# Layer 2 of a two-layer cross-attention: where partial sums are added, how the image part joins the heads, and which function tables ScalarE uses

## The chip, the cores and the metric

The kernel runs on one core of a Trainium2 chip. The core has TensorE (PE in the profile; its weight loads are a row of their own, PEld), VectorE (DVE), ScalarE (ACT), GpSimd (POOL) and SyncE (SP, which here only issues DMAs). [...] The metric is the device time of one execution in microseconds. Three runs of the kernel before took 1663.47, 1673.33 and 1674.31 us, median 1673.33.

## The reference

Two attention layers follow each other, on 16 batches of 256 tokens with 320 channels, 20 heads of 16, and a context of 256 tokens with 512 channels, whose last tokens are the image tokens (four of them in layer 2). The change concerns layer 2:

```python
probs_t = softmax(q @ k_text.T * attn_scale)           # per head
text_out = probs_t @ v_text
qsem = probs_t @ text_ehs                              # 512 wide, per head and token
qsem = qsem / max(norm(qsem), EPS)
sem = qsem @ (ip_ehs / max(norm(ip_ehs), EPS)).T
probs_ip = softmax(q @ k_ip.T * attn_scale + 0.5 * sem)
out = text_out + (probs_ip * spatial_mask) @ v_ip
out = out @ W_out + b_out + residual
```

The norm of `qsem` is never formed from its 512 columns. With the Gram matrix G of the context (context times its transpose) the squared norm is p' G p for a row p of probabilities. The kernel computes that form.

## The kernel before, in words

All matrix products run in fp32r. Where more precision is wanted a value is split into a rounded part (made by an ACT copy) and a rest (made by a DVE or POOL subtraction), and products of the parts are summed; `halves` and `split` do this. Layer 1 runs in slots 0 to 79, layer 2 in slots 80 to 159, one slot for four heads of one batch, five slots per batch. `slot1(k)` writes the work of a slot in layer 2 for PE by hand: scores and transposed scores of two halves of the tokens (`both1`, L775 and L780), the norm (`norm1`, L814), the sums over tokens (`attend1`, L826 and L828), the maxima (`maxima1`, L792). Between these, `fill` issues steps of background tasks whose times are due: keys, values and Gram blocks of a coming batch (`keys1`, `tokens1`), its queries (`open1`), and for a finished batch the image softmax (`image_softmax`) and the output projection (`close1`, which calls `finish`). A task is a generator; each `yield` ends a step, and a list of times in slots says when each step is due. PE runs exactly in the order written. The order on the other engines is made by a list scheduler at build time, within the dependencies.

The places that matter:

- *Norm.* For each slot and each of two pairs of heads (u = 0 and 1) `rounded1` leaves the rounded exponentials in `ctb` (ACT, L804) and P minus that in `wt` (POOL, L805). `norm1` multiplies Gram blocks by the rounded part into a PSUM bank, in two groups n = 0 (four matmuls) and n = 1 (three), and DVE multiplies the bank by `wt` into `wt` (L816). After n = 1 the two products are added in SBUF (L818), by POOL for u = 0 and by DVE for u = 1. One slot later `attend1` sums them over tokens with a matmul by a column of ones (L828), behind the value products (L826), into the same bank.
- *Score maxima.* DVE takes the maximum of each score row (L781); the next score matmuls (L780) need that bank again, and L792 turns the maxima for the subtraction inside the exponentials' matmul.
- *Image part.* After a batch's last slot `gather` transposes the heads' results into `hT`, 128 x 3 x 256, and `image_softmax` prepares the image probabilities: a logarithm and an exponential (L897, L898) for the reciprocal root, POOL sums (L902 to L909), a DVE maximum (L907), another exponential (L911). `close1` multiplies them by the image values in three matmuls (L936); DVE adds each into `hT` (L937). Then `split` makes the rounded part of all 768 columns in one ACT copy (L511), the rest of the first 512 in one DVE subtraction (L512), and with one DVE multiply-add (L513) the last 256, whose channels 64 to 127 hold the rest of channels 0 to 63. The output projection (L522) reads the five pieces.
- *Gram block.* `tokens1` builds the blocks of G once per batch; block 5 is scaled by two on DVE (L489).
- *Tables.* ACT loads a function table when a function is not in the loaded set. Before, this stands ahead of a logarithm (L897) and again ahead of the exponential after it (L898).

PSUM tiles of the tags "X", "T" and "P" (at most three, two and one at a time) share six banks; which bank a tile gets is settled at build time.

Of the kernel before, what the change touches and what calls it, by code (L numbers as in the profile page):

```python
# [9 lines left out]
FR = mybir.dt.float32r  # L10
AF = mybir.ActivationFunctionType
ALU = mybir.AluOpType
# [4 lines left out]
B = 16  # L17
S = 256
# [30 lines left out]
def xattn2(  # L49
# [27 lines left out]
    nc = tc.nc  # L77
# [21 lines left out]
    def buf(tag, shape, dtype=F32, bufs=1, name=None):  # L99
        if tag in ("wB", "wD", "vr", "raw"):  # L100
            return sb.tile(shape, dtype, tag=tag, name=name or tag, bufs=bufs)
        size = 1
        for d in shape[1:]:
            size *= d
        if tag not in slots:
            slots[tag] = [0, dtype] + [const_tile([128, max(size, words.get(tag, 0))], f"{tag}_{i}", dtype) for i in range(bufs)]
        n, kind, *ring = slots[tag]
        assert kind == dtype and len(ring) == bufs, tag
        slots[tag][0] += 1
        t = ring[n % bufs][: shape[0], :size]  # L110
        names = "abcd"[: len(shape) - 1]
        if len(names) > 1:
            t = t.rearrange(f"p ({' '.join(names)}) -> p {' '.join(names)}", **dict(zip(names, shape[1:])))
        return t
# [17 lines left out]
    def queued(inst, *behind):  # L132

        for other in behind or [anchors.get(inst.ins.engine)]:
            if other is not None:
                tc.add_manual_dep(
                    inst.ins, other.ins.name, mybir.DependencyInfo(mybir.DependencyClass.NoSync, mybir.DependencyReason.DATA), reason="order"
                )
        return inst
# [225 lines left out]
    def weights1():  # L365


        cipn = buf("rawc", [128, 512], bufs=2, name="cipn")[:BI]
        dma(cipn, cip_d)
        yield  # L370
        sq = buf("rawc", [128, 512], bufs=2, name="sq")[:BI]
        nc.vector.tensor_mul(sq, cipn, cipn)
        nrm = rn[:BI, 0:1]
        nc.vector.tensor_reduce(nrm, sq, axis=AX.X, op=ALU.add)
        yield
        nc.scalar.activation(nrm, nrm, AF.Sqrt)
        yield
        nc.vector.tensor_scalar_max(nrm, nrm, 1e-12)
        nc.vector.reciprocal(nrm, nrm)
        dg = buf("rawc", [128, 512], bufs=2, name="dg")[:BI]  # L380
        nc.vector.memset(dg[:, BI : BI + 128], 1.0)
        nc.vector.tensor_scalar_mul(dg[:, :BI], ident[:BI, :BI], nrm)
        yield
        rp = bank()
        mm(rp[:, :BI], dg[:, BI : BI + 128], dg[:, :BI], start=True, stop=True)
        nc.vector.tensor_copy(rn, rp[:, :BI])
        cip = w1["cip"] = buf("kst", [128, 2, 4, BI], FR, bufs=SIZES["KST"], name="cip")
        raw = buf("rawc", [128, 4, BI], bufs=2, name="cipT")
        dma(raw, cipT_d.rearrange("(k p) n -> p k n", p=128))
        yield  # L390
        halves(cip[:, 0], cip[:, 1], raw, nc.vector, True)
        yield
# [69 lines left out]
    def tokens1(b):  # L462
        ct = ct1[b]
        V, G = v1t[b % 2], gmt[b % 2]
        vc = vcols(V, V1W)
        for t, lo, sc in ((0, 0, 1.0), (1, DUP, tmask[:, 2:3])):
            vp = bank()[:, :320]
            prod(vp, lambda s, k: ct(s, k)[:, lo : lo + 128], w1["v"], 4)
            nc.scalar.activation(vc[:, t, :, 0:16], vp.rearrange("p (h d) -> p h d", d=D), AF.Copy, scale=sc)
            yield  # L470
        rnb = rn[:, 4 * b : 4 * b + 4].unsqueeze(1).to_broadcast([128, H, NIP])
        for t, lo in ((0, 0), (1, DUP)):
            g = bank()[:, :S]
            prod(g, lambda s, k: ct(s, k)[:, lo : lo + 128], ct, 4)
            ip = g[:, T1:S].unsqueeze(1).to_broadcast([128, H, NIP])
            if t == 0:
                nc.vector.tensor_mul(vc[:, 0, :, 17:21], ip, rnb)
                nc.scalar.copy(G[:, 0, :], g[:, 0:128])
                nc.scalar.copy(G[:, 1, 4:], g[:, 128:T1])
                nc.vector.tensor_sub(G[:, 4, :], g[:, 0:128], f(G[:, 0, :]))  # L480
            else:
                tm = tmask[:, 2:3]
                nc.vector.scalar_tensor_tensor(vc[:, 1, :, 17:21], ip, tm, rnb, op0=ALU.mult, op1=ALU.mult)
                nc.scalar.activation(G[:, 2, :], g[:, 0:128], AF.Copy, scale=tm)
                nc.scalar.activation(G[:, 3, 4:], g[:, 128:T1], AF.Copy, scale=tm)
                nc.vector.scalar_tensor_tensor(
                    G[:, 5, :], g[:, 0:128], tm, f(G[:, 2, :]), op0=ALU.mult, op1=ALU.subtract
                )
                nc.vector.tensor_scalar_mul(G[:, 5, :], f(G[:, 5, :]), 2.0)  # L489
                nc.vector.scalar_tensor_tensor(  # L490
                    G[:, 6, 4:], g[:, 128:T1], tm, f(G[:, 3, 4:]), op0=ALU.mult, op1=ALU.subtract
                )
            yield
        return V, G
# [12 lines left out]
    def split(src, neg, eng, tag):  # L507

        hl = buf(tag, [128, 5, S], FR)
        order = queued if tag == "hq" else lambda inst: inst  # L510
        order(nc.scalar.copy(hl[:, 0:3], src))  # L511
        order(eng.tensor_sub(hl[:, 3:5], src[:, 0:2], f(hl[:, 0:2])))  # L512
        order(nc.vector.scalar_tensor_tensor(hl[:, 2], f(hl[:, 2]), neg, src[:, 2], op0=ALU.mult, op1=ALU.add))  # L513
        return hl
# [226 lines left out]
        return hT  # L741

    def finish(l, b, hT, resid, extra=None):
        if extra is not None:
            yield from extra(hT)
        if l:
            yield
        hh = split(hT, tmask[:, 6:7], nc.vector, "ho")
        results["taken", l * B + b] = True
        yield  # L750
        y = resid

        def evac(m, pp):
            nc.vector.scalar_tensor_tensor(
                y[:, m], pp, bo[:, l, m : m + 1], resid[:, m], op0=ALU.add, op1=ALU.add
            )

        yield from project(l, wo[l], hh, evac)
        return y
# [49 lines left out]
    def norm1(k, u, n):  # L809

        gm = get("t1", k // NG - B)[1]
        yp = bank().rearrange("p (h t) -> p h t", h=2)
        for i, (gb, kt) in enumerate(blocks[n]):
            mm(yp, gm[:, gb], R[k, u][:, kt], start=i == 0, stop=i == len(blocks[n]) - 1)  # L814
        w = W[k, u]
        nc.vector.tensor_mul(w[:, n], yp, w[:, n])  # L816
        if n:
            (nc.vector if u else nc.gpsimd).tensor_add(w[:, 0], w[:, 0], w[:, 1])  # L818

    def attend1(k):  # L820
        b, g = divmod(k - NS, NG)
# [108 lines left out]
    def close1(b):  # L930
        hT, (pT, bd) = results["gathered", 1, b], get("i1", b)

        def extra(hT):
            for p in range(3):
                ip = bank()[:, :S]
                mm(ip, bd[:, p * 128 : (p + 1) * 128], pT, start=True, stop=True)  # L936
                nc.vector.tensor_add(hT[:, p], hT[:, p], ip)  # L937
                yield

        y = yield from finish(1, b, hT, load(x1d[b], "xc"), extra)  # L940
        dma(out_d[b].rearrange("(k p) t -> p k t", p=128), y)
# [25 lines left out]
    def task(key, times, make, *needs):  # L967
        tasks[key] = [times, 0, make, needs, len(tasks)]
# [38 lines left out]
    def shifted(n, *times):  # L1007

        return [RAMP(n + t) for t in times]
# [23 lines left out]
    for b in range(B):  # L1033
        n = NS + 5 * b
        task(("k1", b), shifted(n, -7, -6.67, -6.33, -5.67, -5, -4.67), lambda b=b: keys1(b), ("w2",), *([("t1", b - 1)] if b else []), *([("w4", 1)] if b > 2 else []))
        task(("t1", b), shifted(n, -3.67, -3, -2.67, -2.33), lambda b=b: tokens1(b), ("k1", b), ("w3", b % 2))
        task(("o1", b), shifted(n, -7.67, -7, -6.67, -5.33, -4.33, -4), lambda b=b: open1(b), ("w7",), ("c0", b), *([("o1", b - 1)] if b else []))
        task(("i1", b), shifted(n, 6.67, 6.67, 6.67, 6.67, 7.33, 7.33, 7.67, 7.67, 8, 8.33), lambda b=b: image_softmax(b, NG - 1 if b == B - 1 else 0), ("gathered", 1, b), ("taken", B + b - 1), *([("i1a",)] if b == B - 1 else []))
        task(("c1", b), shifted(n + (1.67 if b > B - 3 else 0), 8.67, 8.67, 8.67, 8.67, 9, 9.67, 11.67, 13), lambda b=b: close1(b), ("i1", b), ("w4", 1))
    task(("i1a",), [2 * NS + 0.1], lambda: image_softmax(B - 1, 0, NG - 1), ("i1", B - 2))  # L1040
    spread = lambda t, d, n: [t + d * i for i in range(n)]
    thirds = lambda n, t: [t + i // 3 + (0.2, 0.6, 1.0)[i % 3] for i in range(n)]
# [153 lines left out]
```

## Time and profile before

| | |
|---|---|
| runs | 1663.47, 1673.33, 1674.31 us (median 1673.33) |
| profiled execution, span from first to last instruction | 1663.4 us |
| matmul busy / weight-load busy | 1533.5 us / 1222.9 us |
| DVE / POOL / ACT busy | 1317.2 / 1202.2 / 877.7 us |
| mean granted TensorE clock | 0.974 |

The profiled execution's own time is its span and some tenth of a microsecond: it agrees with the lowest of the three runs. Rows by line give the engine, the operation, output and input tiles, shapes and count, then busy time and the mean duration in ns, then the idle time of the engine just ahead of them and what ended it. Waits read "who, waiting for whom: total us, times, longest". Matmul ends are modelled, so a busy PE may hide short stalls. The first instruction of layer 2's norm runs at about 770 us; from there to about 1600 us the work repeats with each batch.

### The profile page before, as it was taken

To read this page: it belongs to the slowest core of one execution; us is meant where nothing else is said; L and a number is where in the kernel's file an instruction comes from. 1 tells how busy PE (TensorE), PEld (TensorE's weight loads), DVE (VectorE), ACT (ScalarE), POOL (GpSimd) and SP (SyncE) were. 2 spreads that over 40 slices of the span, in tenths; PEclk is the share of its full clock that TensorE was granted. 3 is DMA by queue.
4 is the path that set the end of the run, shared out by engine and by line. 5 is a ranking of instruction groups with operands and counts; after the bars stand their busy time and mean duration, and the time that the engine had idled before them with its cause. 6 is when DMAs were issued, how large, how long until landed. Compare 5 with 4: busy or idle time off the path is not lost.

```text
span 1663.4 us, 35253 instructions
## 1 busy us (share of the span) xinstructions
PE 1533.5 (92%) x12666; PEld 1222.9 (74%) x12666; DVE 1317.2 (79%) x2484; ACT 877.7 (53%) x1865; POOL 1202.2 (72%) x1194
## 2 busy tenths in 40 slices
PE   7789999999999898789999999999999999999996
PEld 6677888787888786677677777777777777777754
DVE  5367676777776677867889889889888998899885
ACT  5344444444444445435656555655565556556563
POOL 3458787878787767767778777867876777777784
PEclk9899999999999899899999999999999999999998
DMA  7867777777776676655424342434243324332301
GB/s 219 218 196 212 200 215 197 211 202 213 198 220 194 192 203 185 159 178 153 147 66 129 106 128 90 133 106 129 85 131 113 120 89 131 117 105 82 115 17 43
DMA packets 247739, 247.43 MB, mean 149 GB/s; under 512 B 31050, under 2 KB 231468, under 8 KB 247564
## 3 DMA queue, kind: packets, MB, share of 16 engines
q1 hardware_dynamic: 245356, 243.87, 49.7%
q8 instruction: 101, 1.65, 0.4%
q10 hardware_dynamic: 2208, 1.30, 0.3%
q14 instruction: 74, 0.61, 0.1%
HBM read 121.21 MB, written 88.18 MB: 126 GB/s over the span
## 4 chain that ended last, share of the span: by engine, by line
PE 55%; DVE 18%; DMA 10%; POOL 4%; SPq 4%; issue 3%; ACT 3%; ACTq 0%; DVEq 0%; POOLq 0%
PE X L205 14%; PE X L814 12%; PE X L522 8%; PE P L709 5%; DMA qs<-qd 4%; SPq L82 4%; PE S L649 3%; DVE mn L781 3%; DVE wt L818 3%; PE T L673 3%; PE P L826 3%; PE T L775 2%; DVE wt L816 2%; PE P L828 2%; DVE ho L512 2%
## 5 line engine op out<-in xcount | busy, mean ns | idle before, releaser
L679 POOL TENSOR_TENSOR P<-P,rs 128x512 f32<-128x512 f32 x320 | 412.2, 1309 | 169.3 <-ACT P L676 169.0
L805 POOL TENSOR_TENSOR wt<-P,ctb 128x512 f32<-128x512 f32 x320 | 451.0, 1424 | 76.0 <-ACT ctb L804 75.6
L814 PE MATMUL X<-ctb,gm 128*128 128x512 f32 x1120 | 329.3, 412 | 2.5 <-DVE wt L816 2.5
L676 ACT ACTIVATE P<-T 128x512 f32<-128x512 f32 x320 | 176.1, 595 | 233.8 <-PE T L673 128.3
L786 ACT ACTIVATE P<-T 128x512 f32<-128x512 f32 x320 | 173.9, 597 | 138.8 <-PE T L775 137.4
L816 DVE TENSOR_TENSOR wt<-X,wt 128x512 f32<-128x512 f32 x320 | 215.3, 678 | 17.4 <-PE X L814 16.9
L804 ACT ACTIVATE ctb<-P 128x512 fp32r<-128x512 f32 x320 | 195.3, 632 | 61.5 <-PE X L814 60.8
L814 PEld LDWEIGHTS X<-ctb,gm 128*128 128x128 f32 x1120 | 189.6, 188 | 48.6 <-DVE wt L816 5.2
L781 DVE TENSOR_REDUCE mn<-S 128x4 fp32r<-128x1008 f32 x160 | 191.1, 1194 | 0.6 <-PE S L780 0.6
L651 DVE TENSOR_REDUCE mn<-S 128x4 fp32r<-128x716 f32 x160 | 142.6, 891 | 0.0
L673 PE MATMUL T<-qs,ks 127*128 127x256 f32 x640 | 112.5, 296 | 22.9 <-DVE tmp L726 9.9
L709 PE MATMUL P<-P,vr 128*32 128x256 f32 x1920 | 129.3, 405 | 0.0
L649 PE MATMUL S<-ks,qs 125*128 125x256 f32 x640 | 117.7, 308 | 11.7 <-DMA ks<-kd 4.6
L649 PEld LDWEIGHTS S<-ks,qs 125*128 125x128 f32 x640 | 88.7, 195 | 48.6 <-issue 38.4
L522 PE MATMUL X<-ho,wF 128*128 128x256 f32 x768 | 112.4, 289 | 6.7 <-DVE ho L512 2.9
L522 PE MATMUL X<-hq,wE 128*128 128x256 f32 x768 | 111.9, 289 | 5.8 <-ACT hq L511 3.1
L818 POOL TENSOR_TENSOR wt<-wt 128x512 f32<-128x512 f32 x80 | 103.3, 1292 | 14.8 <-DVE wt L816 14.7
L673 PEld LDWEIGHTS T<-qs,ks 127*128 127x128 f32 x640 | 93.0, 198 | 28.0 <-DVE tmp L726 11.9
L522 PEld LDWEIGHTS X<-ho,wF 128*128 128x128 f32 x768 | 103.0, 194 | 12.5 <-DVE ho L512 4.6
L522 PEld LDWEIGHTS X<-hq,wE 128*128 128x128 f32 x768 | 102.7, 194 | 11.4 <-POOL hq L512 5.2
L650 DVE TENSOR_REDUCE mn<-S 128x4 fp32r<-128x308 f32 x160 | 74.9, 468 | 44.1 <-PE S L649 43.6
L818 DVE TENSOR_TENSOR wt<-wt 128x512 f32<-128x512 f32 x80 | 106.1, 1326 | 2.1
(201 smaller groups left out, 2973.9 us busy)
## 6 DMA issues: line engine op xcount, KB each, us to landing
qd<-q SPq DMA_DIRECT2D x96, 384.0 KB
qs<-tph SPq DMA_DIRECT2D x64, 308.0 KB
kd<-kst SPq DMA_DIRECT2D x73, 256.0 KB
rawc<-in_cT_dram SPq DMA_DIRECT2D x60, 256.0 KB
qs<-qd SPq DMA_DIRECT2D x80, 192.0 KB
ks<-kd SPq DMA_DIRECT2D x80, 192.0 KB
ks<-kd SPq DMA_DIRECT2D x160, 96.0 KB
qs<-qd SPq DMA_DIRECT2D x160, 96.0 KB
```

The lines of the kernel that those rows point to most:

```text
L205: last = mm(out, lhs(a, k), rhs(b, k), start=i == 0, stop=i == len(terms) - 1)
L522: mm(pp, w(s, k, slice(m * 128, (m + 1) * 128)), a[:, t], start=i == 0, stop=i == len(terms) - 1)
L649: mm(sp[:, h], Q[: XROW + T0, h, t * 128 : (t + 1) * 128], K[: XROW + T0, h], start=True, stop=True)
L673: mm(st[p][:, j], K[:KS0, 2 * p + j, t * 128 : (t + 1) * 128], Q[:KS0, 2 * p + j], start=True, stop=True)
L679: anchor(nc.gpsimd.tensor_mul(pt, pt, rs[:, t : t + 1].to_broadcast([128, 2, S])))
L709: mm(pv[32 * s : 32 * s + 32, o : o + S], v[:, vt, h : h + 32], P[k, s // 2][:, t, s % 2], start=vt < 2, stop=vt != 1,)
L781: anchor(nc.vector.tensor_reduce(maxes[k + 2][:, t], sp[:, :, :T1], axis=AX.X, op=ALU.max))
L804: nc.scalar.activation(R[k, u][:, t], P[k, u][:, t], AF.Copy, scale=0.5)
L805: anchor(nc.gpsimd.tensor_sub(W[k, u][:, t], P[k, u][:, t], f(R[k, u][:, t])))
L814: mm(yp, gm[:, gb], R[k, u][:, kt], start=i == 0, stop=i == len(blocks[n]) - 1)
L816: nc.vector.tensor_mul(w[:, n], yp, w[:, n])
L818: (nc.vector if u else nc.gpsimd).tensor_add(w[:, 0], w[:, 0], w[:, 1])
```

## The change

Four edits, all in layer 2 (the table preload stands late in layer 1, where the weights of layer 2 are prepared):

1. In `norm1`, for u = 1 and n = 1, the product stays in its PSUM bank, and DVE adds it from there to the first product. For u = 0 nothing changes.
2. In `close1` each image matmul's bank receives `hT` plus itself (DVE, in PSUM); the rounded part is copied from the bank (ACT), and the rest is taken from the bank (DVE), piece by piece. `hT` is no longer written, and `finish` calls `split` only in layer 1. The eight step times of `close1` become six: the three pieces are due at 8.67, 9 and 9.33 slots, where before all three were due at 8.67 and the split at 9.
3. Gram block 5 is doubled by an ACT copy with a scale.
4. Behind the one square root a table set with both logarithm and exponential is loaded explicitly.

```diff
-        nc.scalar.activation(nrm, nrm, AF.Sqrt)
+        root = nc.scalar.activation(nrm, nrm, AF.Sqrt)
+        queued(nc.scalar.preload_act_table_set("natural_log_exp_and_others"), root)
...
-                nc.vector.tensor_scalar_mul(G[:, 5, :], f(G[:, 5, :]), 2.0)
+                nc.scalar.activation(G[:, 5, :], f(G[:, 5, :]), AF.Copy, scale=2.0)
...
     def finish(l, b, hT, resid, extra=None):
-        if extra is not None:
-            yield from extra(hT)
-        if l:
-            yield
-        hh = split(hT, tmask[:, 6:7], nc.vector, "ho")
+        hh = split(hT, tmask[:, 6:7], nc.vector, "ho") if extra is None else (yield from extra(hT))
...
-        nc.vector.tensor_mul(w[:, n], yp, w[:, n])
+        product = yp if n and u else w[:, n]
+        nc.vector.tensor_mul(product, yp, w[:, n])
         if n:
-            (nc.vector if u else nc.gpsimd).tensor_add(w[:, 0], w[:, 0], w[:, 1])
+            (nc.vector if u else nc.gpsimd).tensor_add(w[:, 0], w[:, 0], product)
...
         def extra(hT):
+            hl = buf("ho", [128, 5, S], FR)
             for p in range(3):
                 ip = bank()[:, :S]
                 mm(ip, bd[:, p * 128 : (p + 1) * 128], pT, start=True, stop=True)
-                nc.vector.tensor_add(hT[:, p], hT[:, p], ip)
-                yield
+                nc.vector.tensor_add(ip, hT[:, p], ip)
+                nc.scalar.copy(hl[:, p], ip)
+                if p < 2:
+                    nc.vector.tensor_sub(hl[:, 3 + p], ip, f(hl[:, p]))
+                    yield
+                else:
+                    nc.vector.scalar_tensor_tensor(hl[:, 2], f(hl[:, 2]), tmask[:, 6:7], ip, op0=ALU.mult, op1=ALU.add)
+            return hl
...
-        task(("c1", b), shifted(n + (1.67 if b > B - 3 else 0), 8.67, 8.67, 8.67, 8.67, 9, 9.67, 11.67, 13), lambda b=b: close1(b), ("i1", b), ("w4", 1))
+        task(("c1", b), shifted(n + (1.67 if b > B - 3 else 0), 8.67, 9, 9.33, 9.67, 11.67, 13), lambda b=b: close1(b), ("i1", b), ("w4", 1))
```

In the built program each engine has as many instructions as these edits say: PE, POOL and SP as before, DVE as many as before in other forms, ACT 14 more (32 copies and 16 doublings more, 34 table loads fewer). Layer 1 keeps its order on PE.

## The prediction

> **What bounds the kernel now.** I read the page first (span, busy times, chain), then one repeat of layer 2 as a stretch of the window view, then the waits, and last the chain inside that stretch.
>
> ```profile
> span 1663.4 us, 35253 instructions
> PE 1533.5 (92%) x12666; PEld 1222.9 (74%) x12666; DVE 1317.2 (79%) x2484; ACT 877.7 (53%) x1865; POOL 1202.2 (72%) x1194
> PE 55%; DVE 18%; DMA 10%; POOL 4%; SPq 4%; issue 3%; ACT 3%; ACTq 0%; DVEq 0%; POOLq 0%
> ```
>
> The busy shares name PE, but 18% of the chain that ended last lies on DVE. Every edit but one table load acts in layer 2, which begins around 770 us. There the work of one batch (five slots) repeats every 56.14 us:
>
> ```profile
> core 0: us, PE busy (x) PEld busy (x) DVE busy (x) ACT busy (x) POOL busy (x), PEclk, DMA share, GB/s
> 1021.30:1077.44 56.14, 54.14 (x431) 41.02 (x430) 50.61 (x83) 32.71 (x67) 42.18 (x44) 1.00 0.36 113
> ```
>
> PE 54.1 and DVE 50.6 of 56.1 us: two engines near their ends, each waiting for the other in a fixed order. The granted clock is 1.00, and DMA engines are busy a third of the time, so neither limits. What PE loses stands in the waits (total us, times, longest):
>
> ```profile
> PEld P L828 <- DVE wt L818: 42.8, 64, 3.3
> PE P L828 <- DVE wt L818: 17.7, 22, 2.8
> PEld X L792 <- DVE mn L781: 16.5, 17, 2.0
> PE X L792 <- DVE mn L781: 10.4, 14, 1.6
> PEld S L780 <- DVE mn L781: 9.5, 15, 1.0
> PE S L780 <- DVE mn L781: 6.3, 14, 0.8
> PEld X L814 <- DVE wt L816: 5.2, 13, 0.4
> DVE m L907 <- POOL a L904: 25.3, 17, 2.3
> ```
>
> All the PE waits are waits for DVE. By the matmul rows they cost 17.7 + 10.4 + 6.3 = 34.4 us; by the weight-load rows 42.8 + 16.5 + 9.5 + 5.2 = 74.0 us. A matmul's end is modelled and overlaps the next, so part of a stall hides in "busy": the true loss lies between, and I hold it nearer to 74, because 64 of the 80 slots have their L828 held by the DVE add L818. The chain inside the repeat shows the two worst places (start, length, what):
>
> ```profile
> 1021.35 0.70 DVE wt L816
> 1022.07 1.31 DVE wt L818
> 1023.38 1.68 DVE ho L512
> 1025.06 1.43 DVE ho L513
> ...
> 1027.58 1.16 DVE mn L781
> ...
> 1051.07 0.04 ACT L898
> 1051.11 1.26 issue
> ...
> 1053.89 0.32 DVE m L907
> 1054.21 1.12 DVE mn L781
> ...
> 1055.38 0.22 PE X L792
> ```
>
> First place: the product L816, the add L818 and the split L512, L513 stand in one row on DVE, and the score maximum L781, which the next score matmuls need, is late by them. Second: the image softmax's Exp waits for a table load (the 1.26 us called issue), POOL's sums come after it, DVE stands at L907 for them, and behind L907 stands the maximum that L792 needs.
>
> **The change, part by part.** Rows by line (busy us, mean ns, then idle):
>
> ```profile
> L818 DVE TENSOR_TENSOR wt<-wt x80: 678/1344/1830, 777.9 to 1639.0; 128x512 f32<-128x512 f32 x80
> L816 DVE TENSOR_TENSOR wt<-X,wt 128x512 f32<-128x512 f32 x320 | 215.3, 678 | 17.4 <-PE X L814 16.9 <-PE X L792 0.5
> L512 DVE TENSOR_TENSOR ho<-hT,ho 128x512 fp32r<-128x512 f32 x32 | 48.6, 1517 | 17.3 <-ACT ho L511 17.3
> L513 DVE SCALAR_TENSOR_TENSOR ho<-ho,tmask,hT 128x256 fp32r<-128x256 f32 x32 | 31.9, 997 | 0.0
> L489 DVE TENSOR_SCALAR gm<-gm 128x128 fp32r<-128x128 f32 x16 | 19.8, 1234 | 0.0
> L937 DVE TENSOR_TENSOR hT<-hT,X 128x256 f32<-128x256 f32 x48 | 17.3, 411 | 2.2 <-PE X L936 2.2
> L531 DVE TENSOR_TENSOR q<-X,q 128x256 fp32r<-128x256 f32 x96 | 40.3, 420 | 27.0 <-ACT q L530 26.4
> L754 DVE SCALAR_TENSOR_TENSOR xc<-X,bo,xc 128x256 f32<-128x256 f32 x96 | 45.0, 469 | 4.1 <-PE X L522 3.3
> L530 ACT CAST q<-X 128x256 fp32r<-128x256 f32 x96 | 35.9, 374 | 85.0 <-PE X L522 81.5 <-issue 2.9 <-DMA qs<-mt 0.6
> L511 ACT CAST ho<-hT 128x768 fp32r<-128x768 f32 x32 | 26.6, 832 | 13.7 <-DVE hT L937 11.1 <-DVE hT L739 2.3 <-issue 0.2
> L484 ACT ACTIVATE gm<-X,tmask 128x128 fp32r<-128x128 f32 x16 | 5.6, 350 | 0.0
> L897 ACT ACT_TABLE_LOAD x17 | 21.8, 1283 | 0.3
> ```
>
> *The add (80 times, five per batch).* With both inputs in SBUF it takes 678 ns at best and 1344 in the median. With one input in PSUM the same shape takes 678 (L816). No row has a 128x512 DVE result written to PSUM, so the new product is bounded by 678 and 1344, at which it would eat the whole saving; nothing in the rows makes it cheaper than 678, and I take 678, since L816 differs only in the output. The new add has the form of L816: 678, bounds the same. Saving 1.344 - 0.678 = 0.67 us, 3.3 us per batch. A second effect is cover: the product's bank stays taken until the add has run, about 0.7 us longer; other banks are free then in most slots of the built order, and it counts with the waits below.
>
> [...]
>
> *The image part (once per batch).* Before: three adds, one ACT copy, one subtraction, one multiply-add: DVE 3 x 0.411 + 1.517 + 0.997 = 3.75. After: three adds in PSUM (L937: 0.411), two subtractions with a PSUM input (L531: 0.420), one multiply-add with one (L754: 0.469): 2.54. Saving 1.2 us per batch. The bounds: 0, and 1.8 by the L512 and L513 of the chain quoted above, which took 0.6 more than these means. ACT pays 3 x 0.374 - 0.832 = 0.29, beside idle time of its own.
>
> It adds waits. In the built order the second subtraction stands directly behind the second add on DVE, and the final multiply-add directly behind the third; each waits for ACT's copy in between: 0.374 and two hand-overs, some 0.5 us of DVE idle, 1.0 per batch. If ACT has two exponentials in front, 1.2 more each. Behind the first stands the transpose L872 and then the maximum L781; behind the second the key split L148 and the next L816. On ACT, behind the waiting copies stand the exponentials L786 and the roundings L804. And the PSUM banks of the three image matmuls are now held until the split is done; in the built order the third image matmul, a key product and an L814 group each wait for such a bank. From the third image matmul a key product and two short groups lie on PE ahead of that L814 group; the chain add, copy, multiply-add is 0.41 + 0.37 + 0.47 = 1.25, and a maximum and a product (1.16 + 0.68) stand ahead of it on DVE: 3.1 us in all, most of it beside that PE work. I take 0.7 us of PE loss per batch for all new waits, one hand-over of 0.5 and a little of the queue; the ends are 0 and 3.1. The image matmuls move from one step to three; no DMA is added. SP keeps its 1141 instructions: some in layer 2 change places with neighbours, under a DMA share of 0.36.
>
> *The Gram block (once per batch).* DVE loses 1.234, ACT gains about 0.35 (L484, the same size from PSUM; from SBUF the nearest row is L511 with six times the columns, 0.832, the upper end). The block is first used by L814 more than two slots later, and that work covers it; without the cover it would cost its 0.35.
>
> *The tables.* The built order has 3 loads for 37; the 17 on L897 and as many on L898 are gone, 34 x 1.283 = 43.6 us of ACT. Where ACT idles, that is worth nothing; it counts at the second place above, 1.28 per batch, and at the end:
>
> ```profile
> 1637.85 1.28 ACT L897
> ...
> 1644.73 1.28 ACT L898
> ```
>
> These are the first and the last of four loads in the chain that ends the kernel, two on L897 and two on L898, 5.1 us. [...]
>
> **The sum.** Per batch DVE then needs 50.6 - 3.3 - 1.2 - 1.2 + 1.0 idle = 45.9 us, and PE without its waits 56.1 - 74.0/16 = 51.5: PE bounds the stage alone, and most waits for DVE can go. Of the weight-load waits:
> - L828, 42.8 in 64 waits, mean 0.67. Each shrinks by at most the 0.67 of the add; the longest is 3.3, so they are uneven and some keep a rest. I take 30.
> - L792, 16.5: the chain ahead of it loses 1.28 and one add. I take 14.
> - L780, 9.5: the add and split ahead of it lose 0.67 + 1.2. I take 8.
> - L814, 5.2: it waits for banks. I take 1.
>
> Together 53. Against it the new waits, 16 x 0.7 = 11. At the end 5 from the loads and 1 from the pipelined split. 53 - 11 + 6 = 48 us off. The profiled execution took its span and about 0.1 around it (the lowest run is 1663.47): 1663.5 - 48 = 1615. The median of the runs is 1673.3, 10 above that execution; the next median can lie 0 to 10 above its own profile, and I put it at 1619.
>
> **The rivals.**
> - *The new hand-overs take back half.* For: two more DVE-to-ACT-to-DVE hand-overs per batch in front of a maximum. Against: ACT is busy 32.7 of 56.1. At 2.2 instead of 0.7 us per batch: 24 us less gain, 1643.
> - *The add stays long*, because the product's PSUM write costs what was saved (1344 instead of 678), or because the longer waits of L828 have another cause, such as POOL's own add. Then L828 keeps its 42.8 and the 30 is not won: 1649. Against: L816. [...]
> - *All 74 go* and nothing new comes: 1663.5 - 74 - 6 = 1583, 4 up for the median as above: 1588. Against: two coupled engines at 46 and 51 of a period seldom run without a wait.
> - *Slower: the held banks.* Place: the third image matmul and the two matmul groups that wait for a split bank, in every batch. Each costs PE directly what DVE and ACT trail by; with ACT two exponentials and two roundings behind (2 x 0.597 + 2 x 0.632 us, rows below) each wait is 2.5 us. The gain is used up at (53 + 6)/16 = 3.7 us per batch, between one such wait and two. With two, 4.9: 16 x 4.9 - 59 = 19 us slower, 1663.5 + 19 + 4 = 1687; with all three, 1726. Against: ACT's half idle time.
>
> ```profile
> L786 ACT ACTIVATE P<-T 128x512 f32<-128x512 f32 x320 | 173.9, 597 | 138.8 <-PE T L775 137.4 <-PE X L814 1.4
> L804 ACT ACTIVATE ctb<-P 128x512 fp32r<-128x512 f32 x320 | 195.3, 632 | 61.5 <-PE X L814 60.8 <-POOL hsn L880 0.6
> ```
>
> - *It doesn't do what it says*: excluded for the tables and the product, which stand in the built order; the rest is size.
>
> **How the numbers follow.** 1619 with its surroundings (1602 to 1634) 0.60; half taken back (1635 to 1647) 0.14; add stays long (1640 to 1656) 0.08; all gone (1588 to 1601) 0.08; within 1% of 1673 (1657 to 1690), where rivals one and two add up, 0.06; slower 0.04. About 1% is what a measurement of this kernel can tell from no change; its runs spread by 0.65%. Faster 0.90, same 0.06, slower 0.04. The range leaves out the last two and the outer ends of two others: 1596 to 1648.
>
> **What would show it.** The add's row from PSUM near 678 ns, the product's too; the wait of PEld L828 for DVE under 15 us; L792 and L780 nearly gone from PE's waits; L907's wait for POOL well under 25; the repeat near 53 us with DVE near 45 busy; no table loads behind the softmax. Wrong it would be if the waits of L828 stay with POOL named, if PE's X matmuls wait for the new subtractions, or if the product's row is over 1 us.

## The result and the profile after

The changed kernel takes 1627.36 us (median of four runs, 1626.01 to 1632.38); the kernel before took 1671.02 us in four runs. The ratio is 0.9746, with a 95% interval of 0.9719 to 0.9773: faster by 2.5%. The forecast was 1619 us with a range of 1596 to 1648, so the sign and the range hold, and the time came out 8 us longer. The ratios here and below are formed from all runs of both kernels and differ a little from the quotients of the medians. In the profiled execution the span fell from 1663.4 to 1624.2 us.

First the page of the changed kernel: the span, the busy times and the shares of the chain that ended last. Then one repeat of layer 2 from the window view (start and end, length, then the busy time of each engine with its instructions, the clock, the DMA share and GB/s).

```profile
span 1624.2 us, 35326 instructions
PE 1510.9 (93%) x12666; PEld 1220.1 (75%) x12666; DVE 1232.3 (76%) x2484; ACT 839.1 (52%) x1879; POOL 1169.3 (72%) x1194
PE 71%; DMA 11%; DVE 6%; ACT 3%; POOL 3%; SPq 2%; issue 2%; ACTq 0%; POOLq 0%; DVEq 0%
```

```profile
core 0: us, PE busy (x) PEld busy (x) DVE busy (x) ACT busy (x) POOL busy (x), PEclk, DMA share, GB/s
985.13:1038.66 53.53, 52.09 (x429) 40.53 (x427) 44.70 (x84) 30.37 (x68) 40.00 (x44) 1.00 0.42 131
```

A batch takes 53.5 us instead of 56.1, DVE is busy for 44.7 of them instead of 50.6, and DVE's share of the last chain has gone from 18% to 6%, PE's from 55% to 71%. The kernel is bound by PE as the forecast said. Yet 53.5 is well above the 51.5 that PE was said to need without its waits. The groups by line show that most single instructions became what they were priced at:

```profile
L814 DVE TENSOR_TENSOR wt<-X,wt 128x512 f32<-128x512 f32 x240 | 161.7, 679 | 12.4 <-PE X L811 11.2 <-POOL hsn L728 0.6 <-PE X L935 0.6
L814 DVE TENSOR_TENSOR X<-X,wt 128x512 f32<-128x512 f32 x80 | 55.7, 696 | 7.8 <-PE X L811 6.1 <-PE X L789 0.3
L816 DVE TENSOR_TENSOR wt<-wt,X 128x512 f32<-128x512 f32 x80 | 54.2, 678 | 1.6
L802 POOL TENSOR_TENSOR wt<-P,ctb 128x512 f32<-128x512 f32 x320 | 418.4, 1324 | 109.2 <-ACT ctb L801 108.9
L939 DVE TENSOR_TENSOR ho<-X,ho 128x256 fp32r<-128x256 f32 x32 | 13.3, 416 | 6.2 <-ACT ho L937 6.2
L942 DVE SCALAR_TENSOR_TENSOR ho<-ho,tmask,X 128x256 fp32r<-128x256 f32 x16 | 7.6, 478 | 5.8 <-ACT ho L937 5.7
L490 ACT ACTIVATE gm<-gm 128x128 fp32r<-128x128 f32 x16 | 4.9, 304 | 0.0
```

L814 is the product (L816 in the kernel before), L816 the add (before L818), L802 POOL's subtraction (before L805), L939 and L942 belong to the image part, and L490 doubles the Gram block. The add from PSUM takes 678 ns, the product into PSUM 696. Why the add from SBUF had taken 1344 stands in the last section. The two new hand-overs leave DVE idle for 6.2 + 5.7 us. The loss is elsewhere, and the waits show it (who, waiting for whom: total us, times, longest). L826 was L828 and L789 was L792; L523 is the output projection and L491 the last copy of a Gram block.

```profile
PE X L523 <- DVE gm L491: 18.7, 13, 1.4
PEld P L826 <- DVE wt L816: 13.3, 23, 3.3
PE P L826 <- DVE wt L816: 5.4, 7, 2.9
DVE m L905 <- POOL a L902: 3.9, 13, 0.3
PEld X L789 <- DVE mn L778: 1.7, 4, 0.9
PE X L789 <- DVE mn L778: 0.6, 1, 0.6
PEld P L824 <- DVE wt L814: 2.0, 2, 1.8
```

The wait of the sums (L826) fell from 42.8 to 13.3 us, that of L789 from 16.5 to 1.7, those of L780 and L814 are gone: 59.0 us in all by the weight-load rows. But one long line is new: in 13 batches PE waits 1.44 us ahead of a projection group, 18.7 us, for the copy of a Gram block that the projection does not read. Small ones are new too: weight loads wait 2.0 us ahead of the value products (L824, which was L826), and such rows come to 3.7 us more than before. The chain of one batch shows where (start, length, what):

```profile
1002.74 0.24 PE X L811
...
1003.06 0.44 ACT ctb L801
...
1003.62 0.34 ACT gm L485
1003.95 0.26 ACT gm L486
...
1004.24 0.35 DVE gm L487
1004.59 0.27 DVE gm L491
...
1004.99 1.19 PE X L523 x8
```

The only thing that the projection's third group shares with the Gram copies is a PSUM bank: in the built assignment it writes the bank of the second Gram product of a coming batch. That product stands shortly before it on PE, with only a norm group and the turned maxima between them. The copies out of that bank are late, because ACT's (L485, L486) stand behind a rounding (L801) that waits 0.74 us for PE, and DVE's (L487, L491) stand behind ACT's. In the kernel before, the same group took another bank in the built assignment, and its trace has no such wait.

From the first Gram matmul of layer 2 to the end the profiles give 1663.4 - 765.8 = 897.6 us before and 1624.2 - 768.8 = 855.4 after, 42.2 less; the starts are from these two rows:

```profile
L814 PE MATMUL X<-ctb,gm x1120: 387/395/582, 765.8 to 1636.8; 128*128 128x512 f32 x187
```

```profile
L811 PE MATMUL X<-ctb,gm x1120: 387/396/792, 768.8 to 1602.9; 128*128 128x512 f32 x187
```

The 3.0 us by which layer 1 ended later are no part of the change: in the profiles of the other kernels below this start lies between 765.5 and 772.7. "Layer 2" in the table below is this stretch from first Gram matmul to end.

### The profile page after: what moved, and what is told of

Read it like the earlier page. It is cut to its first block, busy times and chain, and to the rows that moved or that the text cites. A ratio compares the mean times of both kernels' runs of the same rounds, so it can differ in the third digit from the quotient of the medians.

```text
span 1624.2 us, 35326 instructions
## 1 busy us (share of the span) xinstructions
PE 1510.9 (93%) x12666; PEld 1220.1 (75%) x12666; DVE 1232.3 (76%) x2484; ACT 839.1 (52%) x1879; POOL 1169.3 (72%) x1194
## 3 DMA queue, kind: packets, MB, share of 16 engines
q1 hardware_dynamic: 245356, 243.87, 51.5%
## 4 chain that ended last, share of the span: by engine, by line
PE 71%; DMA 11%; DVE 6%; ACT 3%; POOL 3%; SPq 2%; issue 2%; ACTq 0%; POOLq 0%; DVEq 0%
PE X L205 19%; PE X L811 17%; PE X L523 9%; PE P L710 5%; PE P L824 4%; PE T L772 4%; DMA qs<-qd 4%; PE S L650 3%; PE T L674 3%; PE P L826 3%; PE S L777 2%; SPq L82 2%; PE X L935 1%; POOL P L680 1%; DMA kd<-kst 1%
## 5 line engine op out<-in xcount | busy, mean ns | idle before, releaser
L802 POOL TENSOR_TENSOR wt<-P,ctb 128x512 f32<-128x512 f32 x320 | 418.4, 1324 | 109.2 <-ACT ctb L801 108.9
L801 ACT ACTIVATE ctb<-P 128x512 fp32r<-128x512 f32 x320 | 195.3, 632 | 60.2 <-PE X L811 59.5
L814 DVE TENSOR_TENSOR wt<-X,wt 128x512 f32<-128x512 f32 x240 | 161.7, 679 | 12.4 <-PE X L811 11.2
L523 PE MATMUL X<-ho,wF 128*128 128x256 f32 x768 | 113.0, 289 | 24.3 <-DVE gm L491 18.7
L523 PEld LDWEIGHTS X<-ho,wF 128*128 128x128 f32 x768 | 102.8, 193 | 32.1 <-issue 21.3
L523 PE MATMUL X<-hq,wE 128*128 128x256 f32 x768 | 111.2, 289 | 6.5 <-ACT hq L512 3.5
L674 PEld LDWEIGHTS T<-qs,ks 127*128 127x128 f32 x640 | 93.2, 198 | 28.4 <-DVE tmp L727 12.0
L523 PEld LDWEIGHTS X<-hq,wE 128*128 128x128 f32 x768 | 103.9, 196 | 10.4 <-ACT hq L512 3.9
L651 DVE TENSOR_REDUCE mn<-S 128x4 fp32r<-128x308 f32 x160 | 75.0, 469 | 45.6 <-PE S L650 45.1
L205 PE MATMUL X<-cta,wA 128*128 128x252 f32 (+1 forms) x720 | 102.5, 289 | 6.4 <-ACT wA L147 5.4
L816 POOL TENSOR_TENSOR wt<-wt 128x512 f32<-128x512 f32 x80 | 103.7, 1296 | 2.5 <-DVE wt L814 2.5
```

The lines of the kernel that those rows point to most:

```text
L205: last = mm(out, lhs(a, k), rhs(b, k), start=i == 0, stop=i == len(terms) - 1)
L523: mm(pp, w(s, k, slice(m * 128, (m + 1) * 128)), a[:, t], start=i == 0, stop=i == len(terms) - 1)
L674: mm(st[p][:, j], K[:KS0, 2 * p + j, t * 128 : (t + 1) * 128], Q[:KS0, 2 * p + j], start=True, stop=True)
L801: nc.scalar.activation(R[k, u][:, t], P[k, u][:, t], AF.Copy, scale=0.5)
L802: anchor(nc.gpsimd.tensor_sub(W[k, u][:, t], P[k, u][:, t], f(R[k, u][:, t])))
```

## The experiments

My theory after the two traces: the waits that went are those forecast, each edit takes its own, and the add brings the new wait, because its bank is held longer and that shifts the assignment of banks at build time. Rival A: only the DVE time that an edit frees counts, wherever it is. Rival B, the forecast's own fear: the new wait comes from the banks that the image part holds. Others are named with the runs. The diffs are against the kernel before for the first four and against the changed kernel for the rest. Each ratio is to runs of the kernel before beside that kernel, on the same chip.

| kernel | median us | ratio, 95% interval | layer 2 in its profile | PE waits for Gram copy | weight loads of the sums wait |
|---|---|---|---|---|---|
| before | 1671.02 | 1 | 897.6 | none | 42.8 |
| changed | 1627.36 | 0.9746 (0.9719-0.9773) | 855.4 | 18.7 | 13.3 |
| add alone | 1652.77 | 0.9903 (0.9876-0.9930) | 885.1 | 18.8 | 16.4 |
| image part alone | 1648.53 | 0.9871 (0.9843-0.9899) | 873.2 | none | 31.0 |
| tables alone | 1657.33 | 0.9919 (0.9891-0.9948) | 880.7 | none | 42.0 |
| Gram block alone | 1670.23 | 1.0002 (0.9983-1.0020) | 899.4 | none | 43.9 |
| without add | 1630.11 | 0.9740 (0.9709-0.9772) | 859.0 | none | 28.4 |
| without image part | 1642.28 | 0.9828 (0.9785-0.9871) | 873.2 | 18.7 | 17.4 |
| without tables | 1639.18 | 0.9819 (0.9781-0.9857) | 867.6 | 18.7 | 12.5 |
| without Gram block | 1625.98 | 0.9734 (0.9706-0.9761) | 856.8 | 18.8 | 13.1 |
| third group at 13.33 | 1616.73 | 0.9675 (0.9647-0.9704) | 849.8 | none | 28.4 |
| third group at 12.67 | 1619.93 | 0.9691 (0.9667-0.9714) | 849.6 | none | 28.6 |
| at 13.33, without add | 1644.38 | 0.9848 (0.9820-0.9876) | 871.8 | none | 43.1 |
| Gram step at -2 | 1604.64 | 0.9610 (0.9587-0.9633) | 835.3 | none | 12.5 |

**Add alone.**

```diff
-        nc.vector.tensor_mul(w[:, n], yp, w[:, n])
+        product = yp if n and u else w[:, n]
+        nc.vector.tensor_mul(product, yp, w[:, n])
...
-            (nc.vector if u else nc.gpsimd).tensor_add(w[:, 0], w[:, 0], w[:, 1])
+            (nc.vector if u else nc.gpsimd).tensor_add(w[:, 0], w[:, 0], product)
```

> Only the norm product that stays in PSUM and its add (u = 1), all else as before. Theory (the add on DVE is what the sums over tokens wait for): the add's row falls from 1344 to about 680 ns, the L828 wait of the weight loads falls from 42.8 to about 15 us, L792 and L780 by a third; and because the bank of the product is held longer, the built bank assignment gives the third group of the output projection the bank of a Gram product, so that PE waits there for DVE's Gram copy, up to 18 us: net 20 to 30 us off, about 1646. Rival A (only DVE's busy time counts, in proportion): 53 of the 93 us of DVE time that the whole change frees, so 24 us off with no wait of its own. Rival B (the new PE wait of the changed kernel comes from the image part's held banks): no wait for the Gram copy here, 35 us or more off.

The gain is 1.0%, some 16 us: less than both theory and rival A gave. The wait for the Gram copy is there with all of its 18.8 us, from the add alone. So rival B falls:

```profile
PE X L522 <- DVE gm L490: 18.8, 13, 1.4
PEld P L829 <- DVE wt L819: 16.4, 22, 3.6
```

The sums' wait (L829 here) shrank by 26 us and the bank took 19 of them back. The maxima gained little: L792 waits 13.6 us, where a third less than 16.5 was expected, and L780 its 9.5 us as before.

**Image part alone.** The diff is edit 2 of the change with its step times.

> Only the image part added and split in PSUM, with its new step times. Theory: the repeat's first critical place loses 1.2 us of DVE, the maxima come earlier: L780's and L792's waits shrink by half, L828's by about 5 us, the end is 1 us shorter: 10 to 18 us off, and no wait of PE for the Gram copy. Rival A (DVE's freed time in proportion, 19 of 93): 9 us off. Rival B (held banks): the same 10 to 18 won, but about 18 lost to a wait of PE for the Gram copy in the output projection, so within 1% of before.

1.3% off, some 21 us, more than expected and the most of the four; no wait for the Gram copy. In its profile L824 is the matmul of the sums:

```profile
PEld P L824 <- DVE wt L814: 31.0, 63, 3.3
PEld X L788 <- DVE mn L777: 14.8, 17, 1.2
```

L780's 9.5 and L814's 5.2 us are gone but for 0.3, and the sums' wait fell by 11.8 us although the add still takes its long time. That was the place quoted in the forecast where product, add and the split's two long instructions stand in one row on DVE. No run separates the new form of the split from its new step times. The end is shorter too: 1639.0 - 1616.5 = 22.5 us from the last Gram matmul, where it was 26.6.

```profile
span 1639.0 us, 35320 instructions
```

```profile
L810 PE MATMUL X<-ctb,gm x1120: 387/396/792, 765.8 to 1616.5; 128*128 128x512 f32 x187
```

**Tables alone.**

```diff
-        nc.scalar.activation(nrm, nrm, AF.Sqrt)
+        root = nc.scalar.activation(nrm, nrm, AF.Sqrt)
+        queued(nc.scalar.preload_act_table_set("natural_log_exp_and_others"), root)
```

> Only the preloaded function table. Theory: L907's wait for POOL falls from 25.3 to about 5 us, L792's wait on PE's loads from 16.5 to under 8, and the end loses four loads, 5.1 us: 12 to 16 us off. Rival A (DVE's freed time counts; this edit frees none): only the end's 5 us. Rival C (half-idle ACT: loads are worth nothing but at the end): the same 5 us.

0.8% off, some 13 us, as the theory had it; both rivals gave 5 at most. DVE's wait for POOL ahead of the maximum (25.3 us before) and the wait of L792, which turns the maxima (16.5 us before; here it is L793), show the path, in the profile of this kernel:

```profile
DVE m L908 <- POOL a L905: 4.2, 13, 0.6
PEld X L793 <- DVE mn L782: 1.4, 4, 0.7
```

The stretch from the last Gram matmul to the end, 1663.4 - 1636.8 = 26.6 us before, became only 2.3 us shorter, 1646.9 - 1622.6 = 24.3, where the four loads in the chain had 5.1:

```profile
L815 PE MATMUL X<-ctb,gm x1120: 387/396/792, 766.2 to 1622.6; 128*128 128x512 f32 x187
```

**Gram block alone.**

```diff
-                nc.vector.tensor_scalar_mul(G[:, 5, :], f(G[:, 5, :]), 2.0)
+                nc.scalar.activation(G[:, 5, :], f(G[:, 5, :]), AF.Copy, scale=2.0)
```

> Only the Gram block doubled on ScalarE. Theory: 1.2 us of DVE per batch at a place where a third of it meets a wait: 2 to 6 us off, that is within 0.5% of before. Rival A (20 of 93 us of DVE time): 9 us off.

Nothing, within 0.2%, though DVE is busy for 1301.3 us instead of 1317.2; the theory's 2 to 6 us aren't seen either, and the sums wait as long as before (43.9 us). DVE time off the path is worth nothing here, and rival A falls here and with the tables, which freed no DVE time and won 13 us.

**Without the add** (product and add as before).

> The changed kernel with the product and its add as before. Theory: L828's wait comes back in good part (20 us or more), the wait of the output projection for the Gram copy (18.7 us in the changed kernel) is gone: 5 to 20 us slower than the changed kernel, about 1640. Rival A (DVE time in proportion): 24 us slower, about 1651. Rival B (the wait comes from the image part): the wait for the Gram copy stays, 30 us or more slower.

The intervals of the changed kernel and of this one lie on each other (0.9746, 0.9740): in the changed kernel the add is worth nothing that can be measured, where the two intervals leave some 7 us open. That is below most of the theory's 5 to 20, and far from rival A's 24. The sums' wait came back to 28.4 us, the wait for the Gram copy went. So in the set of four the add takes 15.1 us off the sums' wait (28.4 - 13.3), where alone it took 26.4, and the bank costs 18.7 us either way.

**Without the image part** (split, sums and step times as before).

> The changed kernel with the image part as before. Theory: the wait for the Gram copy stays (it comes with the add), the split's long DVE row comes back: 6 to 14 us slower than the changed kernel, about 1637. Rival (the hand-overs of the pipelined image part cost what they save): within 4 us of the changed kernel. Rival B: the wait for the Gram copy goes, and with it up to 18 us.

0.8% slower than the changed kernel (0.9828 against 0.9746), some 14 us, the upper end of what the theory had. The hand-overs on ACT don't eat what the image part saves, and the wait for the Gram copy stays, so it isn't the image part's.

**Third group of the projection at another time.**

```diff
-        task(("c1", b), shifted(n + (1.67 if b > B - 3 else 0), 8.67, 9, 9.33, 9.67, 11.67, 13), ...
+        task(("c1", b), shifted(n + (1.67 if b > B - 3 else 0), 8.67, 9, 9.33, 9.67, 11.67, 13.33), ...
```

> The changed kernel, with the output projection's last step due at 13.33 slots in place of 13, which in the built bank assignment takes away the early reuse of the Gram product's bank. Theory (the 18.7 us are a wait for that bank alone): it is gone, and 8 to 18 us are won, to about 1613. Rival D (ACT and DVE are late there by their queues, and the next PE group waits in its place): the wait moves to another line, within 4 us of the changed kernel.

> The same with the step due at 12.67 slots. Theory: as for the later step, 8 to 18 us off the changed kernel, about 1613. Rival D: within 4 us of it.

Both win: 1616.73 and 1619.93. From the ratios it is 0.7% for the later step, some 12 us, and 0.55%, 9 us, for the earlier one, the lower part of the theory's 8 to 18. The 18.7 us are gone, but not all of them are won, and rival D is right about the rest. This is the chain of the same place with the step at 13.33:

```profile
1004.52 0.34 ACT gm L485
1004.86 0.26 ACT gm L486
...
1005.15 0.35 DVE gm L487
1005.50 0.26 DVE gm L491
1005.76 0.60 DVE wt L816
...
1006.40 0.63 PE P L826 x6
```

The late copies stand on DVE in front of the add L816, and the sums' matmuls wait for that add. PE's timeline has the length of this wait, and the window view the repeat:

```profile
1006.40 0.63 PE L826 MATMUL P<-wt,zone 128*32 128x256 f32 x6 [0.54 <-DVE wt L816]
```

```profile
986.06:1039.05 52.99, 52.45 (x430) 40.58 (x428) 44.70 (x84) 30.36 (x68) 39.93 (x44) 1.00 0.39 120
```

So 0.54 us in such a batch stand where the bank cost 1.44. The sums' wait rises from 13.3 to 28.4 us, and the repeat falls by 0.5 us, to 53.0. The profiled execution is the slowest of this kernel's four, 1622.36 us, so its rows show the smaller part of the gain. With the step at 13 the bank's wait had covered this one.

**At 13.33, without the add.**

> The kernel whose last projection step is due at 13.33, with the product and its add as before. It tells what the add is worth where no bank wait stands against it, and whether the later step is worth something by itself. Theory (the add won its DVE time but paid it back at the Gram product's bank): this kernel takes the time of the changed kernel without the add, 1630 within 4 us; the add is then worth 9 to 14 us where the step is moved, and about 0 to 4 where it isn't. Rival (the later step is good by itself, and the add is worth nothing anywhere): within 4 us of 1617.

Neither: 1644.38, which is 14 us slower than with the step at 13 by the medians and 18 by the ratios. The later step is bad by itself. In the kernel without the add the group at 13 had no bank to wait for and gave PE 1.17 us of work while DVE caught up. Moved behind the sums it covers nothing, and the sums' wait grows from 28.4 to 43.1 us. These are rows of PE's timeline (start, length, line) at that place, first with the step at 13, then at 13.33:

```profile
1011.81 1.17 PE L523 MATMUL X<-ho,wF 128*128 128x256 f32 x8
...
1013.79 0.97 PE L825 MATMUL P<-wt,zone 128*32 128x256 f32 x8
```

```profile
1008.45 0.59 PE L825 MATMUL P<-wt,zone 128*32 128x256 f32 x2
1009.75 0.63 PE L825 MATMUL P<-wt,zone 128*32 128x256 f32 x6 [0.71 <-DVE wt L815]
```

So what the add is worth depends on its surroundings: nothing where the group stands at 13 and takes the Gram bank, and 0.9848 - 0.9675 = 1.7%, 29 us, at 13.33. The sums' wait accounts for 14.7 of these (43.1 - 28.4), and layer 2 in the profiles differs by 22.0; where the rest lies is not shown.

**Gram step later.**

```diff
-        task(("t1", b), shifted(n, -3.67, -3, -2.67, -2.33), lambda b=b: tokens1(b), ("k1", b), ("w3", b % 2))
+        task(("t1", b), shifted(n, -3.67, -3, -2.67, -2.0), lambda b=b: tokens1(b), ("k1", b), ("w3", b % 2))
```

> The changed kernel with the projection's step as it is, but the second Gram product of a batch due at -2 in place of -2.33, so one place later in PE's order; in the built bank assignment its bank isn't taken up at once. Theory (the Gram copies stand on DVE in front of the add that the sums over tokens wait for, and PE pays this at the bank or at the sums): with the copies behind that add, both the 18.7 us at the projection and the 14 us at the sums' matmuls in the two moved-step kernels shrink: repeat 52.3 to 53.0 us, 1606 to 1614. Rival (the copies delay whatever add or maximum stands behind them, wherever they are): the wait returns in another slot, 1616 to 1622.

1604.64 us, 0.961 (0.9587 to 0.9633): faster than the kernel before by 3.9% and than the changed one by 1.4%. The theory's 1606 to 1614 was a little too careful. The second Gram product now comes after the slot's add, so its copies stand behind that add on DVE. These are rows of DVE's timeline (start, length, line, then the idle time ahead), and below them the repeat from the window view and the waits:

```profile
1000.71 0.69 DVE L816 TENSOR_TENSOR wt<-wt,X 128x512 f32<-128x512 f32 x1
...
1003.02 0.35 DVE L487 SCALAR_TENSOR_TENSOR gm<-X,tmask,gm 128x128 fp32r<-128x128 f32 x1 [0.77 <-ACT gm L486]
1003.29 0.34 DVE L491 SCALAR_TENSOR_TENSOR gm<-X,tmask,gm 128x124 fp32r<-128x124 f32 x1
```

```profile
930.53:982.52 51.99, 51.99 (x429) 40.55 (x427) 44.59 (x84) 30.56 (x68) 40.09 (x44) 1.00 0.40 121
```

```profile
PEld P L826 <- DVE wt L816: 12.5, 21, 3.5
```

PE is busy for the whole of the 51.99 us, no wait for the Gram copy is left, and the sums wait as little as in the changed kernel. DVE and ACT are as busy as there (44.59 and 30.56 us). The 1.5 us per batch were the position of one step.

**Without tables, and without the Gram block.**

> The changed kernel with the table loads as before. Theory: the score maxima are late again once per batch (L792's wait of the weight loads near 13 us), and the end has its four loads: 10 to 16 us slower than the changed kernel, about 1640. Rival (the other edits gave ACT and DVE the slack to hide the loads): only the end's 3 to 5 us.

> The changed kernel with the Gram block doubled on DVE as before. Alone this edit was worth nothing that could be measured. Theory: the doubling stands on DVE behind the copies that the projection's bank waits for, and in front of the add, which has slack there: within 4 us of the changed kernel. Rival (it stands in front of the last Gram copy): 1.2 us per batch more at the bank, 15 to 20 us slower.

Without the tables 1639.18, 0.7% or some 12 us slower than changed; the row of the maxima is back at 14.8 us. Without the Gram edit no difference (0.9734 against 0.9746). Both as the theory had it.

## Why the prediction was right, and where it wasn't

- **PE bounds layer 2, and the weight-load rows measure its loss.** Right. These rows fell by 59.0 us and the new wait is 18.7: 40.3, and 5.3 at the end make 45.6, less 3.7 for the small new waits 41.9, against 42.2 measured. The same sum for the kernel with the Gram step at -2 gives 57.1 where 62.3 were measured, so it is good to some 5 us. The matmul rows, 34.4 in all before and 5.4 + 0.6 + 18.7 after, would have given 9.7 in place of 40.3. The kernel with the Gram step at -2 runs its repeat in 51.99 us, close to the forecast of 51.5 for PE without waits; in the changed kernel rival 3 (nothing new comes) failed on the bank.
- **The terms of the sum.** L828 30 against 29.5 measured, L792 14 against 14.8, L780 8 against 9.5, L814 1 against 5.2. Close, and with L814 an underestimate, since the split had caused that wait too. That the first agrees is in part luck: it was forecast from the add, and without the add the sums' wait falls by 14.4 us all the same (42.8 - 28.4).
- **Whose gain it is.** This is the step that failed: "Each shrinks by at most the 0.67 of the add" laid the 30 us of the sums' wait at the add's door. The image part alone takes 11.8 us off it, and in the set the add takes 15.1. By the runs alone the edits win 16, 21, 13 and 0 us (add, image part, tables, Gram block), together 51 where all of them win 42, and the add is worth nothing in the set of four. The rows show the overlap: alone, add, image part and tables take 26.4, 11.8 and 0.8 us off the sums' wait, 39.0 together, and the set takes 29.5. The 1.7 us of DVE per batch which the image part frees (1317.2 - 1289.9 = 27.3 us in all) stand where the sums and the maxima wait for DVE, and the 1.0 us of the Gram block (15.9 in all) where nothing does.
- **The new wait.** Taken at 11 us, at the places where the image part holds banks; measured 18.7 at another. The sentence that failed is that the product's bank "stays taken until the add has run, about 0.7 us longer; other banks are free then in most slots of the built order". It looked at the slots beside the product, and the wait came in another group. For the kernels with the add (alone, changed, without image part, without tables, without Gram block), and no kernel without it, have the projection wait for the Gram copy for 18.7 or 18.8 us. That the longer hold turned the assignment is read from the built programs; that the wait hangs on the place of the two groups, which share nothing but the bank, is shown by moving either. Rival 4 (held banks, slower) named the right kind of wait at wrong places; the point from which it decides, 3.7 us per batch, was not reached with 1.44.
- **The add.** Priced right: 678 ns from PSUM and 696 into it, so rival 2 falls, although the sums' wait partly had another cause, which this rival allowed for: it named POOL's own add, and it was the split. Why 678 became 1344 was not in the forecast (last section).
- **The image part.** Two hand-overs, forecast 1.0 us of DVE idle per batch, measured (6.2 + 5.7)/16 = 0.74. The DVE time was mis-sized: the means of L512 and L513, 1517 and 997 ns, mix both layers; between 840 and 1640 us they are 1689 and 1373. So the saving was 1.7 us per batch, near the forecast's bound of 1.8, and not 1.2. Rival 1 falls with the kernel without this part.
- **Gram block.** Priced right on ACT (304 ns where 350 was taken); its DVE time stood in the forecast's 45.9 us for DVE, not in the waits, and it is worth nothing.
- **Tables.** The path over L907 and L792 is right. The tail's 5.1 us were not: the tables alone shorten it by 2.3 us, the image part alone by 4.1. The two together with the rest gave 5.3 where 6 were forecast.
- **The 8 us to the median.** In spans: 48 forecast, 39.2 measured. The new wait cost 7.7 more than taken, the other rows gave 6.0 more and the end 0.7 less, layer 1 of that execution ran 3.0 longer; the remaining 3.4 us are about the 3.7 of the small new waits. The base was off too: the result lists run times 1.8 us above their spans (1626.01 beside 1624.2), so the profiled execution before was at about 1665.2, not at the lowest run. Against that, the median lay 1.4 us above the profiled execution, where 4 had been added.

What stays open: the overlap of 9 us is read from the sums' wait, and no run takes two edits alone to test it; the split in PSUM and its step times were not run apart; nor was it measured what the Gram step at -2 would be worth without the add.

## What to carry to other kernels

A wait is a place, not an engine's total: 27 us of DVE time taken away were worth 21 us at one place, and 16 us at another were worth nothing. Where a buffer is held longer, look in the built program for who gets which bank afterwards; the new wait stood at a group that the edit didn't touch and cost as much as the edit won there. Before an instruction's mean duration is taken as its price, look at its shortest times and at what ran beside the long ones. After such an edit try again the due times of the steps next to the wait, since a third of a slot moved there won half as much as the four edits together.

## What was not expected of the hardware

The 1344 ns of the add are not what two SBUF inputs cost by themselves. These are rows of the timelines (start, length, engine, line): two of the kernel before near the middle, one of it near the end, where no POOL instruction runs beside the add, and two of the changed kernel.

```profile
1021.55 1.28 POOL L148 TENSOR_TENSOR cta<-rawc,cta 128x512 fp32r<-128x512 f32 x1
1022.07 1.31 DVE L818 TENSOR_TENSOR wt<-wt 128x512 f32<-128x512 f32 x1
```

```profile
1638.99 0.69 DVE L818 TENSOR_TENSOR wt<-wt 128x512 f32<-128x512 f32 x1
```

```profile
1025.70 2.53 POOL L802 TENSOR_TENSOR wt<-P,ctb 128x512 f32<-128x512 f32 x2
1025.94 0.69 DVE L816 TENSOR_TENSOR wt<-wt,X 128x512 f32<-128x512 f32 x1
```

In the first pair the add begins while a POOL subtraction runs and ends 0.55 us behind it. In the trace of the kernel before this holds for all 77 adds (of 80) that begin while POOL runs: they end 545 to 587 ns behind the POOL instruction and take 692 to 1830 ns. The other three find POOL idle and take 678 to 693. The split's subtraction in layer 2 (L512) ends 545 to 552 ns behind POOL in 14 batches, and takes 690 and 691 in the two where POOL is idle. The doubling of the Gram block (L489) ends 82 to 87 ns behind POOL in all 16. It works the other way too: the 77 subtractions of POOL (L805) that begin during such an add take 1692 to 1767 ns, against 1292 in the median of 210 others that begin beside no such DVE instruction.

With one input in PSUM this is gone: 78 of the 80 adds of the changed kernel begin while POOL runs and take 646 to 690 ns, and the 21 subtractions (L802) that begin during one take 1273 to 1302. POOL's subtractions took 1424 ns in the mean before and 1324 after, 1340 with the add alone and 1402 in the kernel without the add. So, by these end times, a good part of the DVE time that the first three edits took away was waiting for POOL, which the profile counts as busy: the adds alone gave 51.9 us (106.1 - 54.2 in the rows by line) of 84.9 in all (1317.2 - 1232.3). Why one engine's instruction ends behind the other's, no run here shows.
